# A two-layer relational graph attention kernel: elu's exponential in PSUM, paired transposes of 64-column rests, half-row stores for the last group

## The chip, the cores and the metric

The kernel runs on one core of one Trainium2 chip. The metric is the device time of one execution in microseconds (us). Three runs of the kernel before gave 1726.51, 1728.38 and 1731.38 us, the median 1728.38 us. All traces are of one profiled execution each.

Names of the engines as the profile writes them: PE is TensorE's matmuls, PEld its weight loads, DVE is VectorE, ACT is ScalarE, POOL is GpSimd, SP is SyncE. L12 is line 12 of the kernel before.

## The reference

A graph has 3125 nodes with 768 features each and 53125 edges, sorted by their target node; each edge has one of 3 relations. Two attention layers run over it, then a residual and a layer norm:

```python
def rgat_conv(x, W, q, k, b, src, dst, etype, heads, out_ch, n):
    xr = einsum('nd,rdf->rnf', x, W)          # one product per relation
    oi, oj = xr[etype, dst], xr[etype, src]   # rows of the edges' two ends
    alpha = leaky_relu(oi @ q + oj @ k, 0.2)
    e = exp(alpha - segment_max(alpha, dst)[dst])
    a = e / (segment_sum(e, dst)[dst] + 1e-16)
    return segment_sum(a * oj, dst) + b       # per head
h   = elu(rgat_conv(x, W1, q1, k1, b1, ..., heads=4, out_ch=192))
out = rgat_conv(h, W2, q2, k2, b2, ..., heads=1, out_ch=768)
y   = layernorm(x + out)
```

elu(v) is v for v > 0 and exp(v) - 1 otherwise. The kernel computes it as max(v, 0) + (min(exp(v), 1) - 1).

## The kernel before, in words

**Groups and slots.** The nodes are cut into 25 groups of 128 at most (NB = 25), each with the edges that end in it. A group's edges fill 17 slots of 128 edges (the first group has 14). Of every slot, 128 rows are fetched from a table in HBM by one indirect DMA that POOL issues (`gather_rows`, L485): 422 gathers in each of the two layers.

**Three stages.** Stage 1 makes the table of the first layer (xr for all relations) and the second layer's weights. Stage 2 (`phase2`) is the first aggregation: it gathers rows from `tab1`, sums them by target, applies elu and multiplies h by W2, whose products it stores as rows of `tab2`. Stage 3 (`phase3`) is the second aggregation: it gathers from `tab2`, sums, and ends in layer norm and the store of the output.

**The order of the work** is written out by hand. Each stage makes a list of steps with `when(k, f, ...)`, where k is a place on an axis counted in slots; the list is sorted by k and then emitted. So k sets only the order in which each engine's queue receives its instructions. Every engine works off its queue in that order and waits for what its next instruction needs. The places stand in the tables `STEPS2` and `STEPS3` at the head of the kernel.

**Stage 2, one group b:**

- `alpha`, `turn`, `scan`, `back`, `weigh` and `sums`, in two halves u = 0 and 1 (slots 0 to 7 and 8 on): scores (DVE), their transposes (PE, tile `pa`), running maxima in both directions (DVE, L921 and L923), exponent (ACT, L927), transposes back (PE), the weighted one-hot matrices `sel` (DVE, L963), and the sums by target (PE, tile `acc`). `alpha` is what waits for the gathered rows.
- `e_y` (L1012): divides by the sum of weights and adds the bias: `y`, 128 partitions by 4 windows by 192. Partition 32h + i of window w holds head h of node 32w + i.
- `e_x` (L1023): exp of y on ACT (L1026), into `ey`.
- `e_h` (L1061): three DVE operations (L1063, L1065, L1066): min and minus 1 on `ey` in place; the sum with max(y, 0) for columns 128 to 191 of each window, written a second time behind column 192 of `y`; the same for all 192 columns, in place. So a window's 256 columns hold the 128 first ones, the 64 others, and the 64 others again.
- `h_row` (L1068): four DMAs on SP store h into `tab2`.
- `e_t` (L1078, `turned`, L1034): 8 transposes on PE of 128 columns each into the PSUM tile `pt`: four windows' first 128 columns into its first bank, and four windows' columns 128 to 255 into its second. As the 64 last columns stand there twice, they come out on partitions 0 to 63 and on 64 to 127.
- `e_s`, `e_s2` (`high_parts` L1039, `low_parts` L1050): h is split into a high part (rounded, ACT) and a low part (the remainder, DVE), tile `hT`. For the first bank that is one operation over 128 partitions by 512 on each engine (L1044, L1055), for the second two over 64 partitions by 256 (L1048, L1059).
- `d_products` (L1088): h times W2 in four pieces of 18 matmuls, in two banks `po` by turns; `d_row` (L1112) copies a piece to SBUF (ACT, L1117) and, after the second piece of a row, stores it with one DMA on SP (L1119).

In steady state PE's queue runs: `turn(b, 1)`, the 8 transposes of group b-1, 20 matmuls of group b-2, `back(b, 1)`, 16 matmuls of group b-1, `sums(b, 1)`, `turn(b+1, 0)`, 20 matmuls, `back(b+1, 0)`, 16 matmuls, `sums(b+1, 0)`. DVE's queue runs: `e_h(b-1)`, `alpha(b, 1)`, `scan(b, 1)`, `low_parts(b-1)`, `weigh(b, 1)`, `marks`, `alpha(b+1, 0)`, `scan(b+1, 0)`, `e_y(b)`, `weigh(b+1, 0)`. From group 15 on, 24 steps `move` (L1002, L1003, both DVE) are spread between these; they prepare the row numbers of stage 3. `paced` makes a gather wait until PE has come to a certain place of the order, in stage 2 about 5.5 slots ahead of the gather's own.

**Stage 3, one group b:** the same chain in one half: `a_alpha`, `a_turn`, `a_scan`, `a_exp`, `a_back`, `weigh` at the places `STEPS3["s"]`, counted from the group's last slot, then `sums`. PE also does the products of the group before (`d_part`, tile `D`, seven places from 2.5 on and five from 5.8 on, counted from the same slot): two of these seven lie before place 3.0. The first gather of stage 3 waits for all stores into `tab2`.

Of the kernel before, what the change touches and what calls it, by code (L numbers as in the profile page):

```python
# [21 lines left out]
P = 128  # L22
# [43 lines left out]
def _index(ap):  # L66
# [36 lines left out]
STEPS3 = {"f": -13,  # L103
          "marks": -5,
          "q": (-19, -17.27, -3.5, -2),
          "s": (1.9, 3.0, 3.05, 3.1, 5.6, 5.7, 9.5),
          "round": 0.9,
          "r": (16.7, 16.7, 16.72, 16.75, 19.25, 19.3, 16.71, 16.73, 20.5, 20.6),
          "t": (16.74, 16.78),
# [6 lines left out]
def kernel(  # L116
# [727 lines left out]
    def phase2(work, psum):  # L844
# [166 lines left out]
        def e_y(b):  # L1011
            s = blk[b]  # L1012
            acc = [a[:, :HW].rearrange("p (w f) -> p w f", w=2) for a in s["acc"]]
            rz = work.tile([P, 2, 2], F32, name="rz", bufs=2)
            for c in range(2):
                V.tensor_scalar(rz[:, c], acc[c][:, :, F1], EPS, None, op0=ALU.add)
            V.reciprocal(rz, rz)
            y = s["y"] = work.tile([P, 4, 2 * P], F32, name="y", bufs=1)
            for w in range(4):
                V.scalar_tensor_tensor(y[:, w, :F1], acc[w // 2][:, w % 2, :F1], rz[:, w // 2, w % 2:w % 2 + 1],  # L1020
                                       bias1, op0=ALU.mult, op1=ALU.add)

        def e_x(b):  # L1023
            s = blk[b]
            s["ey"] = work.tile([P, 4, F1], F32, name="ey", bufs=1)
            S.activation(s["ey"], s["y"][:, :, :F1], AF.Exp)  # L1026

        def busy(n):

# [3 lines left out]

        def turned(s, c):  # L1034

            for t in range(4):
                T.transpose(s["pt"][:, c, t * P:(t + 1) * P], s["y"][:, t, c * P:(c + 1) * P], ident)

        def high_parts(s, c):  # L1039

            hT = s["hT"].rearrange("p s t (w i) -> p s t w i", i=32)
            pt = s["pt"][:, c].rearrange("p (w h i) -> p h w i", h=H1, i=32)
            if c == 0:
                S.copy(hT[:, 0, :H1], pt)  # L1044
                return
            for u in range(2):
                p = slice(64 * u, 64 * u + 64)
                S.copy(hT[p, 0, H1:], pt[p, u::2])  # L1048

        def low_parts(s, c):  # L1050

            hT = s["hT"].rearrange("p s t (w i) -> p s t w i", i=32)
            pt = s["pt"][:, c].rearrange("p (w h i) -> p h w i", h=H1, i=32)
            if c == 0:
                V.tensor_sub(hT[:, 1, :H1], pt, hT[:, 0, :H1].bitcast(F32))  # L1055
                return
            for u in range(2):
                p = slice(64 * u, 64 * u + 64)
                V.tensor_sub(hT[p, 1, H1:], pt[p, u::2], hT[p, 0, H1:].bitcast(F32))  # L1059

        def e_h(b):  # L1061
            s = blk[b]
            V.tensor_scalar(s["ey"], s["ey"], 1.0, -1.0, op0=ALU.min, op1=ALU.add)  # L1063
            y, ey = s["y"], s["ey"]
            V.scalar_tensor_tensor(y[:, :, F1:], y[:, :, P:F1], 0.0, ey[:, :, P:], op0=ALU.max, op1=ALU.add)  # L1065
            V.scalar_tensor_tensor(y[:, :, :F1], y[:, :, :F1], 0.0, ey, op0=ALU.max, op1=ALU.add)  # L1066

        def h_row(b):  # L1068

            s = blk[b]  # L1070
            s["rows"] = tab2[b * P * R:(b + 1) * P * R, :].rearrange("(n r) f -> n r f", r=R)
            to = s["rows"][:, WHOLE, :D].rearrange("(w i) (h f) -> h i w f", i=32, h=H1)
            for h in range(H1):
                nc.sync.dma_start(to[h], s["y"][32 * h:32 * h + 32, :, :F1])

        def e_t(b):
            s = blk[b]
# [34 lines left out]
        def d_row(b, p):  # L1112
# [2 lines left out]
            r, c = divmod(p, 2)  # L1115
            n = HW if c == 0 else D + 1 - HW
            S.copy(rows[r][:, c * HW:c * HW + n], po[:, :n])  # L1117
            if c == 1:
                nc.sync.dma_start(s["rows"][:, r, :], rows[r])  # L1119

        def d_tail(b, p):
# [1091 lines left out]
```

## Time and profile before

| what | us |
|---|---|
| median of three runs | 1728.38 |
| the profiled execution, its time | 1726.83 |
| its span, first to last instruction | 1724.9 |
| PE busy (share of the span) | 1640.5 (95%) |
| DVE busy | 1106.6 (64%) |
| POOL busy | 904.8 (52%) |
| ACT busy | 423.8 (25%) |
| mean granted clock of TensorE | 0.979 |

The profiled execution's time is 1.9 us over its span. The span falls into stage 1 (to about 545 us), stage 2 (to about 1128 us), a passage of some 30 us, stage 3 (its gathers run to 1683 us), and a tail. In a row of the timeline the first number is the start in us, the second the time that the row's instructions cover, `xN` their number; the bracket tells how long the engine was idle before and what ended it ("issue" means nothing that the profile shows). In a row of groups the numbers behind the bar are busy us and the mean of one instruction in ns. A matmul's row shows 128 partitions by its columns; the products `D` of stage 3 stand as two records each.

### The profile page before, as it was taken

To read this page: it belongs to the slowest core of one execution; us is meant where nothing else is said; L and a number is where in the kernel's file an instruction comes from. 1 tells how busy PE (TensorE), PEld (TensorE's weight loads), DVE (VectorE), ACT (ScalarE), POOL (GpSimd) and SP (SyncE) were. 2 spreads that over 40 slices of the span, in tenths; PEclk is the share of its full clock that TensorE was granted. 3 is DMA by queue.
4 is the path that set the end of the run, shared out by engine and by line. 5 is a ranking of instruction groups with operands and counts; after the bars stand their busy time and mean duration, and the time that the engine had idled before them with its cause. 6 is when DMAs were issued, how large, how long until landed. Compare 5 with 4: busy or idle time off the path is not lost.

```text
span 1724.9 us, 39077 instructions
## 1 busy us (share of the span) xinstructions
PE 1640.5 (95%) x14233; PEld 1269.5 (74%) x14233; DVE 1106.6 (64%) x4107; ACT 423.8 (25%) x796; POOL 904.8 (52%) x907
## 2 busy tenths in 40 slices
PE   9999999999996999999999999939999999999996
PEld 8999999999995788888888888924444444444443
DVE  5467666676425566666677777465766666666665
ACT  5122222112110111111111111212333333333333
POOL 5100000000007777777777777057777777777770
PEclk9999999999997999999999999969999999999999
DMA  9576766666568999999999999569999999999991
GB/s 329 180 244 210 258 220 210 199 183 203 191 251 281 330 345 355 347 348 348 346 346 356 354 351 351 172 230 324 334 336 340 335 337 338 338 336 340 334 338 39
DMA packets 169368, 500.48 MB, mean 290 GB/s; under 512 B 39891, under 2 KB 82490, under 8 KB 169167
## 3 DMA queue, kind: packets, MB, share of 16 engines
q0 software_dynamic: 70832, 343.91, 56.1%
q1 hardware_dynamic: 90104, 143.89, 25.0%
q10 hardware_dynamic: 8230, 10.10, 1.7%
q8 instruction: 114, 1.87, 0.4%
q14 instruction: 88, 0.71, 0.1%
HBM read 412.96 MB, written 89.63 MB: 291 GB/s over the span
## 4 chain that ended last, share of the span: by engine, by line
PE 69%; DMA 12%; issue 8%; POOL 6%; DVE 4%; ACT 0%; POOLq 0%; DVEq 0%; ACTq 0%; SPq 0%
PE po L56 47%; PE acc L56 13%; PE D L56 4%; DMA waH<-ftab,ridx 3%; DMA waL<-ftab,ridx 3%; POOL waH L485 2%; PE pa L59 2%; PE pt L59 2%; DMA share<-ftab,ridx 1%; DMA extra<-ftab,ridx 1%; POOL waL L485 1%; POOL extra L485 1%; DMA spare_rows<-ftab,ridx 1%; POOL share L485 1%; PE bank L56 1%
## 5 line engine op out<-in xcount | busy, mean ns | idle before, releaser
L485 POOL DMA_INDIRECT extra<-ftab,ridx x296 | 303.3, 1025 | 90.2 <-issue 48.2
L56 PE MATMUL po<-waH,hT 128*128 128x386 f32 (+1 forms) x1200 | 323.1, 344 | 1.0 <-DVE hT L1055 0.8
L56 PE MATMUL po<-waH,xT 128*128 128x386 f32 x1104 | 293.0, 341 | 0.0
L485 POOL DMA_INDIRECT share<-ftab,ridx x209 | 214.2, 1025 | 63.7 <-issue 36.3
L56 PEld LDWEIGHTS po<-waH,hT 128*128 128x128 f32 x1200 | 220.4, 189 | 3.4 <-DVE hT L1055 1.1
L56 PE MATMUL po<-waL,hT 128*128 128x386 f32 (+1 forms) x600 | 207.6, 346 | 0.0
L56 PE MATMUL D<-extra,AT 128*128 128x512 f32 (+1 forms) x576 | 207.2, 503 | 0.0
L56 PEld LDWEIGHTS po<-waH,xT 128*128 128x128 f32 x1104 | 202.4, 189 | 0.5 <-issue 0.4
L56 PE MATMUL po<-waL,xT 128*128 128x386 f32 x552 | 186.9, 339 | 0.0
L598 ACT COPY share<-po 128x386 f32<-128x386 f32 x150 | 72.3, 482 | 371.2 <-PE po L56 298.7
L56 PEld LDWEIGHTS D<-extra,AT 128*128 128x128 f32 x576 | 105.6, 193 | 67.9 <-issue 60.3
L56 PE MATMUL acc<-waL,marks 128*32 128x386 f32 (+1 forms) x860 | 152.8, 490 | 0.0
L56 PE MATMUL po<-wbH,xT 128*128 128x386 f32 (+1 forms) x552 | 147.5, 341 | 1.3 <-DVE wbL L431 1.3
L56 PE MATMUL acc<-waH,marks 128*32 128x384 f32 (+1 forms) x828 | 141.3, 496 | 0.7 <-DVE marks L1359 0.7
L56 PE MATMUL acc<-extra,marks 128*32 128x386 f32 (+1 forms) x564 | 129.5, 487 | 0.0
L485 POOL DMA_INDIRECT waL<-ftab,ridx x108 | 108.1, 1001 | 32.9 <-issue 26.8
L56 PE MATMUL acc<-extra,sel 128*32 128x193 f32 x2736 | 122.6, 331 | 2.3 <-DVE sel L963 2.3
L927 ACT ACTIVATE e<-e 32x128 f32<-32x128 f32 (+2 forms) x50 | 15.5, 310 | 432.9 <-DVE e L926 432.9
L485 POOL DMA_INDIRECT waH<-ftab,ridx x103 | 102.8, 998 | 31.4 <-issue 25.0
L56 PEld LDWEIGHTS po<-waL,hT 128*128 128x128 f32 x600 | 113.7, 190 | 0.6 <-issue 0.3
L762 POOL DMA_DIRECT2D share<-in_L_gnn_W_dram x24 | 12.8, 536 | 188.4 <-DVE w2j L773 117.3
L56 PEld LDWEIGHTS acc<-extra,sel 128*32 128x32 f32 x2736 | 86.7, 111 | 31.4 <-issue 5.8
(312 smaller groups left out, 3078.1 us busy)
## 6 DMA issues: line engine op xcount, KB each, us to landing
ftab<-share SPq DMA_DIRECT2D x150, 193.0 KB
ftab<-r SPq DMA_DIRECT2D x50, 386.0 KB
sT<-dr_d SPq DMA_DIRECT2D x23, 544.0 KB
xb_d<-share SPq DMA_DIRECT2D x25, 384.0 KB
ftab<-y SPq DMA_DIRECT2D x100, 96.0 KB
share<-xb_d SPq DMA_DIRECT2D x25, 384.0 KB
share<-in_x_dram SPq DMA_DIRECT2D x24, 384.0 KB
out_dram<-share SPq DMA_DIRECT2D x24, 384.0 KB
```

Of the source, the lines that this page charges most:

```text
L56: return self.add(self.engine.matmul(to, weights, moving, **more), to, moving)
L59: return self.add(self.engine.transpose(to, a, unit), to, a)
L485: return G.indirect_dma_start(out=to, out_offset=None, in_=tab, in_offset=_index(i[:, j:j + 1]), bounds_check=NP * R - 1, oob_is_err=False)
L598: S.copy(o[:, :HW], po[:, :HW])
L762: G.dma_start(w2[i][p:p + n], l2["W"][r, at:at + n, :])
L927: S.activation(e, e, AF.Exp)
```

## The change

- `e_x`: `ey` lies in PSUM, in the two banks of `pt`, instead of SBUF. `e_h` works on it there.
- `e_h`: the second sum goes to a tile of its own, `rest`, 128 partitions by 256 (four windows by 64); `y` is 192 columns wide.
- `turned`: the rests are transposed two windows at a time: 2 transposes in place of 4, so 6 per group in place of 8. The rest of an even window comes out on partitions 0 to 63, that of an odd one on 64 to 127.
- `high_parts` and `low_parts`: for the rests four operations over 64 partitions by 128 on each engine, in place of two over 64 by 256. Two of the four read one half of the partitions and write the other.
- `d_row`: for the last group every half row is stored by a DMA of its own, as soon as it is copied.
- `STEPS3["s"]`: `a_turn`, `a_scan` and `a_exp` move from places 3.0, 3.05 and 3.1 to 2.2, 2.35 and 2.4.

```diff
-          "s": (1.9, 3.0, 3.05, 3.1, 5.6, 5.7, 9.5),
+          "s": (1.9, 2.2, 2.35, 2.4, 5.6, 5.7, 9.5),
...
-            y = s["y"] = work.tile([P, 4, 2 * P], F32, name="y", bufs=1)
+            y = s["y"] = work.tile([P, 4, F1], F32, name="y", bufs=1)
+            s["rest"] = work.tile([P, 2 * P], F32, name="rest", bufs=1)
...
         def e_x(b):
             s = blk[b]
-            s["ey"] = work.tile([P, 4, F1], F32, name="ey", bufs=1)
-            S.activation(s["ey"], s["y"][:, :, :F1], AF.Exp)
+            ey = psum.tile([P, 2, 512], F32, name="pt", bufs=1)
+            s["ey"] = ey.rearrange("p c (w f) -> p (c w) f", w=2)[:, :, :F1]
+            S.activation(s["ey"], s["y"], AF.Exp)
...
         def turned(s, c):
 
-            for t in range(4):
-                T.transpose(s["pt"][:, c, t * P:(t + 1) * P], s["y"][:, t, c * P:(c + 1) * P], ident)
+            if c == 0:
+                for t in range(4):
+                    T.transpose(s["pt"][:, 0, t * P:(t + 1) * P], s["y"][:, t, :P], ident)
+                return
+            for t in range(2):
+                T.transpose(s["pt"][:, 1, t * P:(t + 1) * P], s["rest"][:, t * P:(t + 1) * P], ident)
+
+        def rests(s, k):
+
+            hT = s["hT"].rearrange("p s t (m q i) -> p s t m q i", q=2, i=32)
+            pt = s["pt"][:, 1, :2 * P].rearrange("p (m t u i) -> p t m u i", m=2, u=2, i=32)
+            for u in range(2):
+                for q in range(2):
+                    yield hT[64 * u:64 * u + 64, k, H1:, :, q], pt[64 * q:64 * q + 64, :, :, u]
...
-            for u in range(2):
-                p = slice(64 * u, 64 * u + 64)
-                S.copy(hT[p, 0, H1:], pt[p, u::2])
+            for to, rest in rests(s, 0):
+                S.copy(to, rest)
...
-            for u in range(2):
-                p = slice(64 * u, 64 * u + 64)
-                V.tensor_sub(hT[p, 1, H1:], pt[p, u::2], hT[p, 0, H1:].bitcast(F32))
+            for (to, rest), (high, _) in zip(rests(s, 1), rests(s, 0)):
+                V.tensor_sub(to, rest, high.bitcast(F32))
...
-            V.scalar_tensor_tensor(y[:, :, F1:], y[:, :, P:F1], 0.0, ey[:, :, P:], op0=ALU.max, op1=ALU.add)
-            V.scalar_tensor_tensor(y[:, :, :F1], y[:, :, :F1], 0.0, ey, op0=ALU.max, op1=ALU.add)
+            V.scalar_tensor_tensor(s["rest"].rearrange("p (w f) -> p w f", w=4), y[:, :, P:], 0.0, ey[:, :, P:], op0=ALU.max, op1=ALU.add)
+            V.scalar_tensor_tensor(y, y, 0.0, ey, op0=ALU.max, op1=ALU.add)
...
             S.copy(rows[r][:, c * HW:c * HW + n], po[:, :n])
-            if c == 1:
+            if b == NB - 1:
+                f = slice(c * HW, (c + 1) * HW)
+                nc.sync.dma_start(s["rows"][:, r, f], rows[r][:, f])
+            elif c == 1:
                 nc.sync.dma_start(s["rows"][:, r, :], rows[r])
```

More of the change, by code (lines that the diff above doesn't have):

```diff
@@ L1017, in e_y @@
             V.reciprocal(rz, rz)
-            y = s["y"] = work.tile([P, 4, 2 * P], F32, name="y", bufs=1)
+            y = s["y"] = work.tile([P, 4, F1], F32, name="y", bufs=1)
+            s["rest"] = work.tile([P, 2 * P], F32, name="rest", bufs=1)
             for w in range(4):
-                V.scalar_tensor_tensor(y[:, w, :F1], acc[w // 2][:, w % 2, :F1], rz[:, w // 2, w % 2:w % 2 + 1],
+                V.scalar_tensor_tensor(y[:, w], acc[w // 2][:, w % 2, :F1], rz[:, w // 2, w % 2:w % 2 + 1],
                                        bias1, op0=ALU.mult, op1=ALU.add)
@@ L1073, in h_row @@
             for h in range(H1):
-                nc.sync.dma_start(to[h], s["y"][32 * h:32 * h + 32, :, :F1])
+                nc.sync.dma_start(to[h], s["y"][32 * h:32 * h + 32])
         def e_t(b):
```

## The prediction

> **What bounds the kernel now.** I read the page's slices first, then the busy time by stage.
>
> ```profile
> span 1724.9 us, 39077 instructions
> ...
> PE   9999999999996999999999999939999999999996
> ```
>
> ```profile
> 602.00:1128.00 526.00, 525.44 (x6076) 455.74 (x6076) 358.60 (x1106) 99.74 (x232) 371.48 (x361) 1.00 0.93 331
> 658.00:680.80 22.80, 22.80 (x278) 19.66 (x274) 14.83 (x49) 4.26 (x10) 17.47 (x18) 1.00 0.97 362
> 1131.00:1683.00 552.00, 509.45 (x3768) 240.68 (x3770) 372.09 (x1686) 184.21 (x307) 422.64 (x422) 0.96 0.94 332
> ```
>
> The columns are length, then busy us of PE, PEld, DVE, ACT and POOL, granted clock, DMA share, GB/s. From 602 to 1128 us PE has work all the time: stage 2 is as long as what stands in PE's queue. In stage 3 PE has 42 us without work, so something else sets its length. POOL's rows by themselves tell what:
>
> ```profile
> 519.67:1083.21 563.54, 435.21 (x422) 0.98 0.96 344
> 1131.84:1682.86 551.02, 422.64 (x422) 0.96 0.94 332
> ```
>
> Length, POOL busy, clock, DMA share and GB/s for the gathers alone. Between two gathers POOL is idle 0.30 us (rows below), so 422 gathers that never wait take 422 x 0.30 more than their busy time: 549 us in stage 3, and it lasts 551. Stage 3 is as long as POOL's issues: whatever is spared or added inside it shows only in its tail. In stage 2 the same sum is 562 of 563.5 us, so POOL looks like a bound there too. The timeline of one group shows why it is none:
>
> ```profile
> 835.91 1.00 POOL L485 DMA_INDIRECT share<-ftab,ridx  x1 [0.30 <-issue]
> 837.21 1.64 POOL L485 DMA_INDIRECT share<-ftab,ridx  x1 [0.30 <-DVE y L1065]
> ```
>
> ```profile
> 859.99 1.61 POOL L485 DMA_INDIRECT share<-ftab,ridx  x1 [0.30 <-DVE y L1065]
> ```
>
> ```profile
> 837.02 0.96 DVE L1066 SCALAR_TENSOR_TENSOR y<-y,ey 128x768 f32<-128x768 f32 x1
> ```
>
> 17 gathers of 1.30 us are 22.1, and one in each group is stretched by 0.64 under elu's large sum on DVE: 22.74, while the group lasts 859.99 - 837.21 = 22.78 us. Every group POOL gains 0.64 on PE and is held by 0.64 at the same DVE instruction; it is locked to PE's pace. Free of that it could go at 22.1 us a group. So stage 2 is PE's, stage 3 POOL's.
>
> **Fewer transposes.**
>
> ```profile
> L59 PE MATMUL pt<-fident,y x200: 270/273/273, 565.1 to 1111.2; 128*128 128x128 f32 x100
> ```
>
> ```profile
> 841.03 1.04 PE L59 MATMUL pt<-fident,y 128*128 128x128 f32 x8
> ```
>
> Eight transposes cover 1.04 us and one lasts 0.273, so one starts every (1.04 - 0.27) / 7 = 0.11 us. Two fewer spare PE 0.22 us a group. PE is the bound from 602 us on; groups 2 to 24 have their transposes after that: 23 x 0.22 = **-5.0 us**. POOL and DMA must then keep 22.55 us a group; POOL can, and the row 658 to 680.8 shows DMA at 362 GB/s where 22.55 us asks for about 1% more than now.
>
> **elu in PSUM.** What DVE's three operations then cost is bounded by these rows:
>
> ```profile
> L390 DVE COPY t<-pt 128x768 f32<-128x768 f32 x3 | 2.9, 957 | 2.9 <-PE pt L59 2.9
> ...
> L1420 DVE SCALAR_TENSOR_TENSOR share<-acc,half,share 128x768 f32<-128x768 f32 x50 | 50.3, 1007 | 1.7 <-ACT share L1415 0.8
> ...
> L1063 DVE TENSOR_SCALAR ey<-ey 128x768 f32<-128x768 f32 x25 | 14.3, 571 | 0.9 <-ACT ey L1026 0.9
> ```
>
> The first operation goes from 0.57 to 0.96 us at most (the copy of 768 columns from PSUM); the large sum from 0.96 to 1.01 (the sum with one operand in PSUM). Operations on PSUM overlap the next one's start, so I take +0.25 us a group, between 0 and +0.45. ACT's exp into PSUM has no row of its own; it ends while DVE is still at `sel`, so it is free. What hides the 0.25 is DVE's lead over the next turn on PE. Where the moves stand in between, there is none left:
>
> ```profile
> 931.99 0.18 DVE L907 COPY near<-al 64x28 f32<-64x28 f32 x1
> ```
>
> ```profile
> 932.23 0.29 PE L59 MATMUL pa<-fident,near 128*36 128x128 f32 x1
> ```
>
> That transpose starts when DVE is done. For this group and its neighbours from 16 on, and the turn that follows the rests' longer work, I charge **+0.5 us** together (0 to 1.2).
>
> The gain on POOL: in the row L1420 above one operand lies in SBUF and one in PSUM, and 50 such sums leave stage 3's gathers at 422.64 / 422 = 1.00 us. Stage 2's took 435.21, so 14 us of stretch stand there, most of it at elu. The Trainium skill, SBUF — State Buffer, section Who interferes with whom, says that a VectorE instruction with two inputs in SBUF contends with a GpSimd instruction that reads SBUF, and one with at most one such input does not; the trace agrees (1.64 against 1.00 us). Taken alone, that rule would make POOL's freedom worth up to the 14 us. PE's row says it is worth something only before 602 us, where PE still waits for rows. There the chain of waits reads
>
> ```profile
> 594.38 7.15 DMA extra<-ftab,ridx
> ```
>
> and ahead of this gather four were stretched under elu:
>
> ```profile
> 559.26 1.25 POOL L485 DMA_INDIRECT share<-ftab,rfirst  x1 [0.30 <-issue]
> 560.81 1.15 POOL L485 DMA_INDIRECT share<-ftab,rfirst  x1 [0.30 <-PE acc L56]
> ```
>
> ```profile
> 583.44 1.38 POOL L485 DMA_INDIRECT share<-ftab,ridx  x1 [0.30 <-PE po L56]
> 585.12 1.15 POOL L485 DMA_INDIRECT share<-ftab,ridx  x1 [0.30 <-issue]
> ```
>
> 0.25 + 0.15 + 0.38 + 0.15 = **-0.9 us** (0 to -1.2).
>
> **The rests in four pieces.** ACT copies them, DVE waits for ACT's last copy, subtracts, and then makes `sel`, for which PE's sums wait:
>
> ```profile
> 843.59 0.75 ACT L1048 CAST hT<-pt 64x256 fp32r<-64x256 f32 x2
> ```
>
> ```profile
> 844.37 0.69 DVE L1055 TENSOR_TENSOR hT<-pt,hT 128x512 fp32r<-128x512 f32 x1 [1.56 <-ACT hT L1048]
> 844.98 0.85 DVE L1059 TENSOR_TENSOR hT<-pt,hT 64x256 fp32r<-64x256 f32 x2
> ```
>
> ```profile
> 845.85 2.02 DVE L963 TENSOR_TENSOR sel<-marks,pa 128x1152 f32<-128x1152 f32 x3
> ```
>
> ```profile
> 848.72 2.17 PE L56 MATMUL acc<-extra,sel 128*32 128x193 f32 x48
> ```
>
> A piece of 64 by 128 has no row. Above it lies that of 64 by 256 (0.37 on ACT, 0.42 on DVE); nearest are operations of 128 columns:
>
> ```profile
> L416 ACT COPY sm<-bank 128x128 f32<-128x128 f32 x9 | 2.4, 266 | 12.0 <-PE bank L56 12.0
> ```
>
> ```profile
> L926 DVE TENSOR_TENSOR e<-pa,B 32x128 f32<-32x128 f32 x25 | 7.0, 278 | 0.9
> ```
>
> The two halves of a row here do not overlap (2 x 0.37 = 0.75, 2 x 0.42 = 0.85), so I let four pieces not overlap either: ACT 4 x 0.28 = 1.1 (+0.37), DVE 4 x 0.29 = 1.18 (+0.33). `sel` comes 0.70 us later, PE 0.22 earlier: 0.92 in all. `sel` is done at 847.87 and its sums start at 848.72, a slack of 0.85. It is more than that, since the sums need only the first of the three instructions at their start. The group at 909 us shows it, where moves stand ahead of `sel`:
>
> ```profile
> 914.76 0.60 DVE L1003 TENSOR_TENSOR pall<-pall 128x425 f32<-128x425 f32 x1
> 915.40 2.02 DVE L963 TENSOR_TENSOR sel<-marks,pa 128x1152 f32<-128x1152 f32 x3
> ```
>
> ```profile
> 917.12 0.37 PE L56 MATMUL acc<-share,sel 128*32 128x193 f32 x4
> ```
>
> `sel` ends at 917.42, 0.30 us after its sums began, and PE did not wait. So an ordinary group has 0.85 + 0.30 = 1.15 us, and 0.92 fits. In a group with a move at this place nothing is left, and PE loses most of the 0.92: 0.8. Such groups are three, with L1003 at 914.76, 960.64 and the last at
>
> ```profile
> 1006.11 0.60 DVE L1003 TENSOR_TENSOR pall<-pall 128x425 f32<-128x425 f32 x1
> ```
>
> 3 x 0.8 = **+2.4 us** (0, if DVE no longer waits for ACT's last copy, to 3).
>
> **The last half rows.** The chain into stage 3 is
>
> ```profile
> 1128.25 2.64 DMA ftab<-r
> ```
>
> ```profile
> ftab<-r SPq DMA_DIRECT2D x50, 386.0 KB
> ```
>
> The last store then carries half the bytes, and the first half is gone before. At the 362 GB/s above, 386 KB need 1.07 of the 2.64 us, so half of them spares 0.5 at most; smaller rows may eat some of it. I take **-0.2 us** (+0.1 to -0.6). SP has two more issues, in gaps while it waits for ACT.
>
> **Turn before the two products.** In stage 3 PE today does two products of the group before, then waits for the scores:
>
> ```profile
> 1666.26 0.27 PE L59 MATMUL pa<-fident,al 128*17 128x128 f32 x1 [0.88 <-DVE al L1313]
> ```
>
> From place 2.2 the turn comes first. It still starts when the rows have landed, and the two products, until now inside the wait, follow it. POOL hides this for all groups but the last. In the tail the chain reads
>
> ```profile
> 1685.77 1.82 PE D L56 x4
> 1687.59 0.22 PE pa L59 x2
> 1687.81 3.87 PE D L56 x10
> ```
>
> Ten records last 3.87, so four cost 1.55, at most 1.82. Behind the turn of group 23, held by its rows, they push everything after it: **+1.6 us** (0 to 2.2). DVE's and ACT's orders stay as they are, and an earlier scan finds PE busy with seven products in place of five.
>
> **Sum.** -5.0 + 0.5 - 0.9 + 2.4 - 0.2 + 1.6 = -1.6 us: 1726.83 to 1725.2 for the profiled execution, which lies 1.55 under the median; on the median 1728.38 that is **1726.8 us**. About 0.3% (5.2 us) is what a measurement here can tell from no change.
>
> **Rivals.**
>
> - *The delays cost nothing.* DVE takes the low parts of the first bank while ACT still copies the rests, and the products behind the turn find another gap: -5.0 - 0.9 - 0.2 = -6.1, 1722.3. For it: the low parts of the first bank need no rests. Against: today's bracket on L1055. 16%.
> - *POOL paces stage 2 after all*, and PE's busy rows hide waits. Freed of some 10 of its 14 us, with the tail's +1.6: 1720. For it: POOL's sum of 562 in 563.5. Against: a matmul that waits shows a gap, and PE shows none. 8%. (It is what the Trainium skill's rule above would give if the gathers alone counted.)
> - *PE's gain is not taken up*, because POOL stays locked (the backward scan too has two operands in SBUF) or DMA is full: 3.4 us over the median, 1731.8. 5%.
> - *Slower: the four pieces cost as much each as the two do now.* Then `sel` is 0.75 + 0.85 = 1.6 later against 1.15 of slack: PE waits 0.45 in each of 23 groups, +10 in place of -5.0 and of the 2.4, with the rest (+1.0) 1739. It decides from about 0.37 us for a piece. For it: two pieces cross from one half of the partitions to the other, for which no PSUM row stands. Against: the 0.27 and 0.28 above. 7%.
>
> **How the numbers follow.** The forecast keeps 64%; its own range runs from 1724 to 1730. The 8-in-10 range takes in the first and the third rival and leaves out the last and most of the second: 1721.5 to 1731.8. Faster by over 0.3% are the first two rivals, 24%; slower the last and a little more, 8%; within, 68%.
>
> **What would show it.** Six transposes of `y` and `rest` a group; gathers in stage 2 near 1.00 us, with no 1.6; the group at 22.55 us until 870 us; three waits of PE for `sel` near 917, 963 and 1008 us; in the tail 14 records of D behind the turn. A group at 22.78 us again would refute the main term, gaps ahead of `acc` in every group would show the last rival, and a tail as short as before would refute the term of the turn.

## The result and the profile after

The changed kernel's median is 1724.99 us over 22 runs (1723.11 to 1728.39), that of the kernel before on the same chips 1728.17 us (1725.15 to 1733.69). The ratio is 0.9984 with a 95% interval of 0.9977 to 0.9991: by the ratio about 2.8 us less, within 0.3%. The forecast was 1.6 us less.

The profiled execution of the changed kernel took 1727.58 us, its span is 1725.8: 0.9 us *more* than the profile of before. The spans must not be compared as they stand. The first gather of stage 2 starts at 523.13 us in place of 519.67; the change touches nothing ahead of it, and further profiles have it anywhere from 519.1 to 525.3. So I compare from that gather on:

| stretch | before | after | difference | forecast |
|---|---|---|---|---|
| first gather of stage 2 to the transposes of group 2 (run-in) | 93.39 | 92.12 | -1.27 | -0.9 |
| those of group 2 to those of group 24 | 497.33 | 495.42 | -1.91 | -1.9 |
| those of group 24 to the first gather of stage 3 | 21.44 | 20.31 | -1.13 | -0.4 |
| gathers of stage 3 | 551.02 | 550.06 | -0.96 | 0 |
| last gather's end to the end (tail) | 42.08 | 44.75 | +2.67 | +1.6 |
| sum | 1205.26 | 1202.66 | -2.60 | -1.6 |

(The forecast of the second row is 22 groups by -0.22, plus 2.9 of delays; two more transposes are in the third.) The windows of after, with the columns of before's:

```profile
602.00:1128.00 526.00, 523.66 (x6098) 454.34 (x6086) 374.64 (x1155) 106.75 (x278) 365.85 (x362) 1.00 0.94 334
660.40:682.96 22.56, 22.56 (x270) 19.42 (x269) 15.86 (x51) 4.58 (x12) 17.19 (x18) 1.00 1.00 365
1131.00:1683.00 552.00, 509.37 (x3762) 242.10 (x3764) 372.53 (x1681) 183.28 (x306) 421.67 (x422) 0.96 0.94 332
```

One group takes 22.56 us in place of 22.80 and PE is busy in all of it. The gathers alone (length, POOL busy, clock, DMA share, GB/s):

```profile
523.13:1082.71 559.58, 426.42 (x422) 0.98 0.97 346
1130.98:1681.04 550.06, 421.68 (x422) 0.96 0.94 333
```

Stage 2's gathers are 9 us less busy than before's 435.21. For the group shown in the prediction, POOL's timeline now has

```profile
837.64 1.00 POOL L485 DMA_INDIRECT extra<-ftab,ridx  x1 [0.30 <-DVE rest L1077]
...
849.61 1.16 POOL L485 DMA_INDIRECT extra<-ftab,ridx  x1 [0.55 <-PE acc L56]
```

The gather beside elu lasts 1.00 us in place of 1.64, and once in this group POOL waits for PE: 0.55 us idle, where the gap between gathers is 0.30. Such waits begin late: the first gap over 0.35 us is

```profile
827.06 1.15 POOL L485 DMA_INDIRECT share<-ftab,ridx  x1 [0.60 <-PE acc L56]
```

and there are ten up to 1050 us, nine of them ended by PE. Ahead of 827 us POOL never waits: 17 gathers take 22.1 to 22.4 us, while PE's groups take 22.55 to 22.60. So POOL gains a lead first, and PE holds it only when it has that lead.

The new operations, by tile `pt` (shortest, median, longest in ns):

```profile
L1061 ACT CAST hT<-pt x100: 255/260/265, 571.6 to 1112.8; 64x128 fp32r<-64x128 f32 x100
L1071 DVE TENSOR_TENSOR hT<-pt,hT x100: 271/288/298, 573.3 to 1114.6; 64x128 fp32r<-64x128 f32 x100
...
L1075 DVE TENSOR_SCALAR pt<-pt x25: 954/958/965, 563.3 to 1107.1; 128x768 f32<-128x768 f32 x25
```

A piece of the rests costs 0.26 us on ACT and 0.29 on DVE; elu's first operation went from 0.57 to 0.96 us. PE's waits behind DVE, none of which before had from 610 us on:

```profile
916.78 4.22 PE L56 MATMUL acc<-share,sel 128*32 128x193 f32 x96 [0.50 <-DVE sel L963]
932.33 0.29 PE L59 MATMUL pa<-fident,near 128*36 128x128 f32 x1 [0.21 <-DVE near L907]
```

```profile
963.20 0.54 PE L56 MATMUL acc<-extra,sel 128*32 128x193 f32 x8 [0.58 <-DVE sel L963]
```

```profile
1009.03 0.53 PE L56 MATMUL acc<-share,sel 128*32 128x193 f32 x8 [0.50 <-DVE sel L963]
```

with a last one for `near` at 1069.69 (0.26). The gaps add up to 2.05 us, but the groups lose more: matmuls in a row overlap when nothing holds them, so a wait costs more than the gap that it leaves. The transpose at 932.33 starts 0.50 us behind the one ahead of it, where the transposes in the prediction start 0.11 apart. Against 22.57 us the four groups with these waits take 23.74, 23.31, 23.26 and 23.00, 3.0 us more in all: 2.2 at `sel` and 0.8 at `near`. The first of them seen from DVE: four pieces, a move, and only then `sel`:

```profile
912.98 1.18 DVE L1071 TENSOR_TENSOR hT<-pt,hT 64x128 fp32r<-64x128 f32 x4
914.20 0.50 DVE L1002 TENSOR_SCALAR pall<-ridx,first_row,moved 128x425 f32<-128x425 int32 x1
914.73 0.60 DVE L1003 TENSOR_TENSOR pall<-pall 128x425 f32<-128x425 f32 x1
915.37 2.02 DVE L963 TENSOR_TENSOR sel<-marks,pa 128x1152 f32<-128x1152 f32 x3
```

And the turn of group 23 with the 14 records of D behind it:

```profile
1665.12 0.27 PE L59 MATMUL pa<-fident,al 128*17 128x128 f32 x1 [0.32 <-DVE al L1328]
1665.62 0.28 PE L59 MATMUL pa<-fident,next 128*17 128x128 f32 x1 [0.23 <-DVE next L1330]
1665.74 5.75 PE L56 MATMUL D<-extra,AT 128*128 128x512 f32 x14
1671.42 0.23 PE L59 MATMUL pa<-fident,e 17*128 17x17 f32 x1
```

Most of the experiments (e1 to e4, e5 and e6, e8 to e11) ran on three chips on which the kernel before takes 1959 to 1986 us, because the gathered rows come in more slowly there; each kernel is compared with the kernel before on its own chip. Line numbers in a row are those of the run's own kernel.

### The profile page after: what moved, and what is told of

Read it like the earlier page. It is cut to its first block, busy times and chain, and to the rows that moved or that the text cites. A ratio compares the mean times of both kernels' runs of the same rounds, so it can differ in the third digit from the quotient of the medians.

```text
span 1725.8 us, 39081 instructions
## 1 busy us (share of the span) xinstructions
PE 1638.3 (95%) x14183; PEld 1267.9 (73%) x14183; DVE 1124.9 (65%) x4157; ACT 431.3 (25%) x846; POOL 894.6 (52%) x907
## 4 chain that ended last, share of the span: by engine, by line
PE 72%; DMA 8%; issue 7%; DVE 6%; POOL 5%; ACT 1%; POOLq 0%; DVEq 0%; ACTq 0%; SPq 0%
PE po L56 46%; PE acc L56 15%; PE D L56 7%; DMA extra<-ftab,ridx 2%; POOL waH L485 2%; DMA waL<-ftab,ridx 2%; PE pa L59 2%; POOL extra L485 1%; PE pt L59 1%; DMA waH<-ftab,ridx 1%; POOL waL L485 1%; DMA spare_rows<-ftab,ridx 1%; POOL share L485 1%; DMA share<-ftab,ridx 1%; DVE junk L1317 1%
## 5 line engine op out<-in xcount | busy, mean ns | idle before, releaser
L485 POOL DMA_INDIRECT extra<-ftab,ridx x296 | 297.6, 1005 | 92.9 <-issue 49.7
L56 PE MATMUL D<-extra,AT 128*128 128x512 f32 (+1 forms) x576 | 202.3, 502 | 0.0
L485 POOL DMA_INDIRECT waL<-ftab,ridx x108 | 107.8, 998 | 32.9 <-issue 26.8
L485 POOL DMA_INDIRECT waH<-ftab,ridx x103 | 102.8, 998 | 31.4 <-issue 26.8
```

The source lines that it names most:

```text
L56: return self.add(self.engine.matmul(to, weights, moving, **more), to, moving)
L485: return G.indirect_dma_start(out=to, out_offset=None, in_=tab, in_offset=_index(i[:, j:j + 1]), bounds_check=NP * R - 1, oob_is_err=False)
```

## The experiments

**How long the gathers hold stage 2 on those three chips.** In a stretch of stage 2 e9 (first row) moves 299 GB/s, the profile of before (second) 349, in columns as above:

```profile
700.00:1150.00 450.00, 418.65 (x4542) 345.30 (x4540) 283.66 (x885) 77.37 (x204) 289.16 (x288) 1.00 0.91 299
```

```profile
680.00:1050.00 370.00, 370.00 (x4382) 319.23 (x4375) 263.32 (x810) 70.23 (x165) 285.87 (x277) 1.00 0.97 349
```

PE is idle for 31 of 450 us. POOL's waits in e8 (us in total, times, longest) have an entry that neither before nor after has:

```profile
POOL extra L485 <- remote: 45.1, 41, 1.9
POOL share L485 <- remote: 33.3, 28, 1.9
```

All ten profiles from these chips have this entry, the four of the other chips (before, after, e7, e12) have none. It names no engine of the core; what holds the gathers there, the trace does not say. A group takes 26.8 to 27.3 us there, so what the change spares on PE is lost in waits for rows. Those runs tell about single operations, the passage to stage 3 and the tail, not about PE's or POOL's pace.

**e2 and e11: elu in PSUM alone** (before, with this edit only):

```diff
-            s["ey"] = work.tile([P, 4, F1], F32, name="ey", bufs=1)
+            ey = psum.tile([P, 2, 512], F32, name="pt", bufs=1)
+            s["ey"] = ey.rearrange("p c (w f) -> p (c w) f", w=2)[:, :, :F1]
```

> The kernel before with one edit: the exponential of elu lies in PSUM. Eight transposes, two pieces for the rests, whole rows and the late turn stay. Theory A: PE paces stage 2, and POOL was only locked to it. Then the 9 us of stretch under elu's large sum go, gaps in which POOL waits for PE come in their place, and the group stays at 22.78 to 22.80 us; only the run-in gains, from the first gather to the transposes of group 2, 92.1 to 92.5 us in place of 93.39; time 1727 (1 us under before). Theory B: POOL paces stage 2 and PE's busy rows hide waits. Then the group falls to 22.2 to 22.4 us and the time to 1715 to 1720. Theory C: the longer operations on DVE delay the turns in the groups with moves: waits for near in the second half of stage 2, up to 0.5 us in all.

> The kernel before with one edit: the exponential of elu lies in PSUM. Theory A: PE paces stage 2, POOL is only locked to it. Then the 9 us of stretch under elu's large sum go, waits of POOL for PE come in their place, the group stays at 22.78 to 22.80 us, and only the run-in gains, 92.1 to 92.5 us from the first gather to the transposes of group 2 in place of 93.39. Time 1 us under before. Theory B: POOL paces stage 2. Then the group falls to 22.2 to 22.4 us and the time to 8 to 12 us under before.

Measured: 1986.39 us against 1985.55, ratio 0.9997 (0.9981 to 1.0014); 1958.31 against 1959.11, 0.9990 (0.9976 to 1.0003). Elu's stretch of the gathers is gone in both. The groups are at 27.2 and 26.8 us, so theories A and B are not told apart. Neither profile has a wait for `near` from 600 us on, so theory C shows nothing here either.

**e3 and e8: elu in SBUF, all else as changed** (the same edit, undone in the changed kernel).

> The changed kernel with one edit undone: the exponential of elu lies in SBUF again, six transposes stay. Theory A: the stretch under elu is only what is left over between POOL and PE, and gets shorter when PE gets faster. Then the group is at 22.57 us as in the changed kernel, the stretch under elu's large sum falls from 0.64 to about 0.43 us a group, and only the run-in is lost: 93.0 to 93.4 us from the first gather to the transposes of group 2 in place of 92.12; time 1 us over the changed kernel, 1726. Theory B: POOL holds PE back by the stretch, and the saving on PE needs elu out of SBUF. Then the group stays at 22.74 to 22.78 us, gathers show 1.6 us as before, and the time is 4 to 5 us over the changed kernel, about 1729.5.

> The changed kernel with the exponential of elu in SBUF again; six transposes stay. Theory A: POOL's stretch under elu is only what is left over between POOL's own 22.1 us and PE's group, and gets shorter when PE gets faster. Then the group is at 22.57 us as in the changed kernel, with about 0.45 us of stretch under elu in each in place of 0.64, and only the run-in is lost: 93.0 to 93.4 us from the first gather to the transposes of group 2 in place of 92.12. Time 1 us over the changed kernel. Theory B: POOL holds PE back by the stretch, and the saving on PE needs elu out of SBUF. Then the group stays at 22.74 to 22.78 us, gathers of 1.6 us stay, and the time is 4 to 5 us over the changed kernel, 1 us over before.

Measured: 1982.07 against 1985.55, 0.9987 (0.9971 to 1.0003); 1957.16 against 1959.11, 0.9980 (0.9967 to 0.9993). Groups at 27.2 and 26.8 us: nothing told apart. e12 has the same edit.

**e12: elu in SBUF, moves at idle places, late turn for the last two groups** (the edit of e3, and these).

```diff
-          "move": 3.3,
+          "move": (9.02, 17.52, 17.57),
...
+          "last": (1.9, 3.0, 3.05, 3.1, 5.6, 5.7, 9.5),
...
-            when(base(late) + STEPS2["move"] + i * (NB - 1 - late) * SL / (NB - 2), move, i + 1)
+            when(base(late + i // 3) + STEPS2["move"][i % 3], move, i + 1)
...
-            for k, f in zip(t["s"], (a_alpha, a_turn, a_scan, a_exp, a_back, weigh)):
+            for k, f in zip(t["s" if b < NB - 2 else "last"], (a_alpha, a_turn, a_scan, a_exp, a_back, weigh)):
```

> The changed kernel with three edits: the 24 moves at the places where DVE waits for PE anyway (three in each of groups 15 to 22), the late turn for the last two groups of stage 3 alone, and the exponential of elu in SBUF again. Where DMA leaves room: for the third edit, theory A: POOL's stretch under elu is what is left over between POOL's 22.1 us and PE's group. Then the group is at 22.57 us as in the changed kernel, the stretch under elu is about 0.45 us in each, and only the run-in is lost, 93.0 to 93.4 us from the first gather to the transposes of group 2 in place of 92.12. Theory B: POOL holds PE back by the stretch; then the group stays at 22.74 to 22.78 us with gathers of 1.6 us. For the others: no wait of PE for DVE in stage 2, a tail of 42.1 to 42.8 us, a stretch of 0.7 us in stage 3's gathers. By A the time is 6.5 to 7 us under before, by B 2 to 3.

Measured, on a chip like that of the first profiles: 1726.20 us over 12 runs against 1729.63, 0.9978 (0.9963 to 0.9993), by the ratio 3.8 us less. Theory A had put the time 6.5 to 7 us under before; that is missed, and theory A is judged by its group and its stretch. In stage 2 PE is without a gap from 658 to 1080 us:

```profile
658.00:1080.00 422.00, 422.00 (x4996) 363.44 (x4998) 312.09 (x980) 86.32 (x226) 325.42 (x318) 1.00 0.98 352
```

Groups 5 to 22 take 22.55 to 22.60 us with elu in SBUF. The gathers beside elu, and the DVE rows over them:

```profile
840.72 1.24 POOL L486 DMA_INDIRECT share<-ftab,ridx  x1 [0.31 <-issue]
842.26 1.15 POOL L486 DMA_INDIRECT share<-ftab,ridx  x1 [0.30 <-issue]
```

```profile
840.52 0.55 DVE L1075 TENSOR_SCALAR ey<-ey 128x768 f32<-128x768 f32 x1
...
841.57 0.96 DVE L1078 SCALAR_TENSOR_TENSOR y<-y,ey 128x768 f32<-128x768 f32 x1
```

The stretch is 0.24 + 0.15 = 0.39 us where before it was 0.64. Theory A holds: the stretch is what is left over between POOL's own pace and PE's, and shrinks with PE's group. It leaves POOL without reserve: its gathers take 562.14 us and it never waits for PE, so late rows are not caught up; PE waits for them at 654.12 (0.90) and 1083.74 us (0.45), and group 4 takes 23.75. From the transposes of group 2 to those of group 24 e12 takes 494.54 us where e7, with the same moves and elu in PSUM, takes 492.35 (one profile each). The run-in is 93.16 us, as A had it.

The tail is 44.21 us, not 42.1 to 42.8. The order did what was expected: from group 23's turn to the next transposes of `A` it took 18.32 us, against 20.15 after. What is longer is the last stretch of D, at a lower granted clock (length, PE busy, clock):

```profile
1707.44:1718.01 10.57, 9.40 (x46) 0.84 0.01 3
```

In e7 the same stretch takes

```profile
1700.30:1709.40 9.10, 7.84 (x46) 1.00 0.02 5
```

1.5 us lie in the clock; without them the tail is 42.7. Six of twelve experiment profiles have it at 0.84 to 0.95 there, with either order; what lowers it is open.

**e1 and e9: the late turn again** (stage 3's places of before) in the changed kernel.

```diff
-          "s": (1.9, 2.2, 2.35, 2.4, 5.6, 5.7, 9.5),
+          "s": (1.9, 3.0, 3.05, 3.1, 5.6, 5.7, 9.5),
```

> The changed kernel with stage 3's turn, scan and exponent back at the places 3.0, 3.05 and 3.1; all else as changed. Measured from the last gather's end to the end of the span (the tail), before had 42.08 us and the changed kernel 44.75; from the first to the last gather of stage 3 they had 551.02 and 550.06. Theory A, the prediction's: the earlier turn costs the tail alone, and POOL hides it elsewhere. Then the tail is 42.1 to 42.8, the gathers stay near 550.1, and the time falls by 1.6 to 2.7 us against the changed kernel, to about 1722.8. Theory B: the earlier turn is also what took 0.9 us of stretch from the gathers under the backward scan (1.28 before, 0.34 after). Then the tail is 42.1 but the gathers take 551.0 again, the stretch under that scan is back near 1.3, and the net is -1.7, about 1723.3. Theory C: the tail hangs on when the last rows land, which scatters; then it stays at 44 or more and the time at 1725.

> The changed kernel with stage 3's turn, scan and exponent back at 3.0, 3.05 and 3.1. Theory A: the early turn costs the tail alone. Then the tail after the last gather is 42.1 to 42.8 us in place of 44.75, the stretch of stage 3's gathers stays near 0.7 us, and the time is 2 us under the changed kernel. Theory B: the early turn also spared the gathers 0.9 us of stretch under the backward scan. Then the tail is the same, but the stretch is back at 1.6 us, and the time is 1 to 1.3 us under the changed kernel.

Measured: 1985.19 against 1985.55, 0.9997 (0.9982 to 1.0012); 1955.74 against 1959.11, 0.9987 (0.9973 to 1.0000). The numbers of the expectations cannot be met there: the last turn comes 15 to 17 us after the last gather, in place of 4.6 to 5.4 on the other chips, and the tails are 54.10 and 54.65 us, against 56.14 to 56.94 in e3, e4, e6 and e8 with the early turn. Part of those 2 us is the clock (e2, with the late turn and the low clock, has 56.28). PE's time from the last turn to its sums is 6.69 to 6.70 us in every profile with the late turn and 8.61 or more with the early one. That shows the order, and is no loss by itself: the early order has in this stretch the four records that the late one has ahead of the turn. What the order costs the tail is shown by e7 and e12, on chips like that of after. The gathers' stretch under the backward scan shows nothing where POOL waits for its queue.

**e5: late turn and elu in SBUF** (both edits from above).

> The changed kernel with two edits undone that lie in different stages: the exponential of elu lies in SBUF again (stage 2), and stage 3's turn, scan and exponent are back at 3.0, 3.05 and 3.1. Where DMA leaves room, as in the profiles of before and of the changed kernel: stage 2, theory A: the stretch under elu is only what is left over between POOL and PE; then the group is at 22.57 us with about 0.43 us of stretch under elu's large sum in each. Theory B: POOL holds PE back by the stretch; then the group is at 22.74 to 22.78 us. Stage 3, theory A: the early turn cost the tail alone; then the tail after the last gather is 42.1 to 42.8 us in place of 44.75, and the gathers stay near 550.1. Theory B: it also spared POOL stretch; then the gathers take 551.0 with 1.3 us of stretch under the backward scan. By A and A the time is that of the changed kernel less 1 us (tail -2, run-in +1).

Measured: 1977.83 against 1980.25, 0.9991 (0.9973 to 1.0009). The group is at 27.2 us and the tail at 54.01: the tail is as short as in e1, the rest is as in e3.

**e4: low parts of the first bank ahead of the rests' high parts.**

```diff
         def e_s(b):
-            for c in range(2):
-                high_parts(blk[b], c)
+            high_parts(blk[b], 0)
+            low_parts(blk[b], 0)
+            high_parts(blk[b], 1)
...
         def e_s2(b):
-            for c in range(2):
-                low_parts(blk[b], c)
+            low_parts(blk[b], 1)
```

> The changed kernel with the low parts of the first bank ahead of the high parts of the rests in the order, so that DVE's subtraction over 128 by 512 waits for ACT's first copy alone and no longer for the fifth. Everything computed as before. DVE can then start 0.61 us earlier after the transposes, but its four pieces still wait for ACT's last copy at 3.62 us behind the transposes: sel ends 0.6 us earlier (its first instruction 6.2 us behind the transposes in place of 6.84). Theory A: the three waits of PE for sel at 916.78 (0.50), 963.20 (0.58) and 1009.03 us (0.50) come from the four pieces. Then all three go, the groups after them fall from 23.74, 23.31 and 23.26 to about 23.1, 22.6 and 22.6 us, and the time falls by about 1.8 us, to 1723.2. Theory B: the moves alone make these waits, or the wait for near behind them takes their place; then the groups stay at 23.2 or more and the time at 1725.

Measured: 1979.66 against 1985.55, 0.9980 (0.9961 to 0.9999), but the edit did not do what I wrote. ACT and PE in one group:

```profile
959.83 1.07 ACT L1061 CAST hT<-pt 64x128 fp32r<-64x128 f32 x4 [0.76 <-DVE hT L1068]
960.92 0.48 ACT L1129 COPY r<-po 128x386 f32<-128x386 f32 x1
```

```profile
961.46 0.44 PE L56 MATMUL po<-waH,hT 128*128 128x386 f32 x1 [0.95 <-ACT r L1129]
```

ACT's four pieces now wait for DVE's subtraction, DVE's pieces wait for ACT, and nothing overlaps: the four pieces on DVE end 0.28 us later in the last group (4.51 in place of 4.23 behind its transposes). ACT's copy of a finished bank moves back with them, and PE waits ahead of its products: 24.4 us in 21 waits from 680 to 1210 us, where e1 has 7.0 in 18 and e3 6.4 in 17. (For 8 of the 21, 8.3 us, the profile names ACT's copy as what ended them; for the rest it names nothing.) The waits for `sel` do shrink, as theory A has it, to 0.5 us in 3 where e1 has 3.2 in 6 and e3 2.6 in 4, but far more is added ahead of the products. So this edit does not hide the pieces; what it would do where rows come in time was not measured. Its ratio lies within the interval of e3's, on the same chip, and has no cause shown.

**e6: the same, and whole rows for the last group.**

```diff
-            if b == NB - 1:
-                f = slice(c * HW, (c + 1) * HW)
-                nc.sync.dma_start(s["rows"][:, r, f], rows[r][:, f])
-            elif c == 1:
+            if c == 1:
```

> The changed kernel with two edits in different places: the low parts of the first bank stand ahead of the high parts of the rests in the order (DVE starts them 0.6 us earlier), and the last group's rows are stored whole again. Where DMA leaves room: theory A for the first edit: PE's waits for sel (0.50, 0.58 and 0.50 us near 917, 963 and 1009 us) go, and the groups after them take 22.6 to 23.1 us in place of 23.74, 23.31 and 23.26; theory B: moves or the wait for near keep them at 23.2 or more. For the second: from the last transposes of stage 2 to the first gather of stage 3 before took 21.44 us and the changed kernel 20.31, of which two transposes are 0.22. Theory A: the half rows made the other 0.9, and whole rows bring 21.2. Theory B, the prediction's size: they made 0.2, the rest is scatter of one store, and it stays at 20.5 or less.

Measured: 1976.62 against 1980.25, 0.9982 (0.9965 to 1.0000). The group's last transposes and the first gather of stage 3 in e6:

```profile
1248.53 0.60 PE L59 MATMUL pt<-fident,y 128*128 128x128 f32 x4
```

```profile
1269.76 0.99 POOL L485 DMA_INDIRECT waH<-ftab,rfirst  x1 [51.08 <-DMA f<-ed_d]
```

That is 21.23 us. With half rows it is 20.31 to 20.39 in ten profiles on at least five chips (20.31 in e4, which differs from e6 by the half rows alone and ran on another chip), with whole rows and eight transposes 21.40 to 21.44 in three. The half rows spare 0.9 us: theory A. The first edit shows as in e4: PE waits 24.5 us in 19 waits ahead of its products.

**e10: moves at idle places and the late turn for the last two groups** (e12 with elu in PSUM).

> The changed kernel with the 24 moves at the places where DVE waits for PE anyway (three in each of groups 15 to 22), and with the late turn for the last two groups alone. Theory A: both gains add up: no wait of PE from 602 us to the end of stage 2's products (-2.9 us), a tail of 42.1 to 42.8 us in place of 44.75 (-2), gathers of stage 3 with 0.7 us of stretch. Then the time is 4.5 to 5 us under the changed kernel and 7.5 to 8 under before, a ratio of 0.9955. Theory B: the tail hangs on the order of all groups, not of the last two; then it stays at 44 and the time is 3 us under the changed kernel.

Measured: 1956.10 against 1959.11, 0.9989 (0.9972 to 1.0006). The tail is 54.09 us, as short as with the late turn in all groups: the last two groups decide, and theory B falls. From 600 us to the end of stage 2 PE waits neither for `sel` nor for `near`. The sum of the gains cannot show there.

**e7: moves at idle places, late turn in all groups.**

> The changed kernel with two edits in different stages. Stage 2: the 24 moves on DVE are no longer spread evenly over groups 15 to 24, but stand three to a group in groups 15 to 22 at places where DVE waits for PE anyway: behind each of the two turns ahead of its scan, and behind the second scan ahead of the low parts. Stage 3: turn, scan and exponent are back at 3.0, 3.05 and 3.1. Where DMA leaves room, theory A: PE's five waits behind DVE (0.50, 0.21, 0.58, 0.50 and 0.26 us at 916.78, 932.33, 963.20, 1009.03 and 1069.69) all go, every group from 3 to 23 takes 22.55 to 22.6 us, and from the transposes of group 14 to those of group 24 it takes 221.6 us in place of 224.55; the tail is 42.1 to 42.8 us in place of 44.75. Together 5 us under the changed kernel, about 1720. Theory B: a move ahead of a scan delays the transposes of the exponents instead, and PE waits there, about 0.3 us in each of the eight groups, so that nothing is won in stage 2; and the early turn had spared stage 3's gathers 0.9 us, so that the time is 1723.5. Where DMA holds the rows back, as in the profiles of e1 to e6, the first part shows nothing and the tail falls by 2.4 us.

Measured, one run on a chip like that of the first profiles: 1722.22 us against one run of the kernel before, 1726.54, 4.3 less. PE has no gap at all:

```profile
658.00:1080.00 422.00, 422.00 (x4995) 363.74 (x4992) 319.43 (x982) 86.05 (x226) 321.82 (x317) 1.00 0.98 352
```

while after had 2.09 us of gaps in the same 422. From the transposes of group 14 to those of group 24 it takes 221.48 us in place of 224.55. A move fits where DVE waits for ACT:

```profile
907.97 0.49 DVE L1002 TENSOR_SCALAR pall<-ridx,first_row,moved 128x425 f32<-128x425 int32 x1
908.49 0.61 DVE L1003 TENSOR_TENSOR pall<-pall 128x425 f32<-128x425 f32 x1
909.93 0.69 DVE L1068 TENSOR_TENSOR hT<-pt,hT 128x512 fp32r<-128x512 f32 x1 [0.83 <-ACT hT L1061]
```

So the delays came from the moves ahead of the longer pieces, 3.07 us in all. The tail is 42.82, 1.93 us shorter. Two things went the other way: stage 3's gathers took 552.15 us, 2.1 more than in after, and the run-in 93.54. About 0.9 of the 2.1 is stretch (1.61 in place of 0.70); the rest is 3 to 4 ns more for each gather. The median gather takes 1.002 us in e7, e10 and e12, the three kernels with the moves at other places, and 0.998 in the other eleven profiles; why is open. From the first gather of stage 2 to the end e7 takes 1201.17 us, 1.5 less than after in these two profiles, where 5 were expected. One run of e7 against one of before is no measurement of the time, and whether e10 beats e7 where rows come in time was not measured.

## Why the prediction was right, step by step

- **Bounds.** Right. PE paces stage 2: freed of the stretch, POOL does 17 gathers in 22.1 to 22.4 us until 827 us and then waits for PE, while PE's groups stay at 22.57 up to the first group with a wait for `sel`. That removes the rival *POOL paces stage 2*. Stage 3 stayed as long as POOL's issues.
- **Fewer transposes, -5.0.** Right: the group fell by 0.22 us, from 22.80 to 22.57 on the mean of groups 3 to 14, and DMA kept up at 365 GB/s. The rival *PE's gain is not taken up* is settled by e12: it is taken up with elu in SBUF as well. DMA can still take it: in three profiles (after, e7, e12) it did.
- **elu in PSUM.** DVE's three operations cost 0.39 us more, not 0.25 (inside the bound of 0.45). The two waits for `near` cost 0.8 us where I charged 0.5; how much of that is elu and how much the rests, no run separates. The gathers run at 1.00 us beside elu, as the row with one operand in PSUM said, and the rule of the Trainium skill that the prediction quotes (SBUF — State Buffer, section Who interferes with whom) agrees there. But the prediction left out a condition of that rule: the section says that a VectorE instruction with at most one input in SBUF does not contend *outside the 2-port perf modes*, and names `tensor_scalar` among the operations that can enter such a mode. The prediction's own rows show why it matters: of its four stretched gathers in the run-in, those at 559.26 and 583.44 us lost 0.25 and 0.38 us under L1063, which has one input. In which mode it ran the trace does not say. In the run-in POOL is spared 1.2 us where I had 0.9: the stretch in the first 56 gathers is 1.75 and 1.68 us with elu in SBUF (before, e12), 0.49 and 0.51 in PSUM (after, e7). Where PE stands then scatters by more: 92.12 us in after and 93.54 in e7 to group 2. So it is shown for POOL, not for the time.
- **The rests, +2.4.** Right in mechanism and size: 2.2. A piece costs 0.26 and 0.29 us against 0.28 and 0.29; `sel` comes 0.67 us later against 0.70; ordinary groups hide it, the three groups named wait. With the waits for `near` it is 3.0 us by the groups and 3.07 by e7, forecast 2.9. *The delays cost nothing* and *the pieces cost as much as now* both fall by these rows.
- **The last half rows, -0.2.** Mis-sized: 0.9. The step that failed is "At the 362 GB/s above, 386 KB need 1.07 of the 2.64 us": the store at the end of stage 2, which stands alone, did not go at the rate of many transfers. The wait for it, of whole rows in e6 and of half rows in after:

```profile
1268.99 0.98 ACT L1297 ACTIVATE qd<-fident,q2f 128x128 f32<-128x128 f32 x3 [2.82 <-DMA ftab<-r]
```

```profile
1130.32 0.99 ACT L1300 ACTIVATE qd<-fident,q2f 128x128 f32<-128x128 f32 x3 [2.01 <-DMA ftab<-r]
```

  0.81 us for 193 KB less is about 240 GB/s, an estimate from these two waits; before, with whole rows on a chip like that of after, has 2.85.
- **Turn ahead of two products, +1.6.** Right in place, under in size: 1.92 us behind the turn of group 23 (18.23 to 20.15 us until the next transposes of `A`). Four records more are 1.7, and D waits 0.2 more for `next`. Another 0.67 of the tail lies ahead of that turn: the rows of group 23 were used 6.23 us after their last gather, before 5.56; this scatters (5.3 to 6.2 in the last groups of e7 and e12 in which PE waited for it). With the late turn the tail is 42.82 in e7 and 42.7 in e12 without its clock, not quite before's 42.08. "POOL hides this for all groups but the last" held.
- **Stage 3's gathers.** The sum has no term for them; they took 0.96 us less, nearly all of it stretch under the backward scan (1.28 to 0.34). The four profiles of chips where rows come in time have 1.63 and 1.61 us of stretch with the late turn (before, e7), 0.70 and 1.00 with the early one (after, e12, but for its last two groups). They agree with an effect of the order, and are too few to show it.

So the mechanisms held, and that the total came out so near is in part luck: the half rows spared 0.7 us more than forecast and the tail lost 1.1 more, which nearly cancel. What is left of the 1.0 us between -1.6 and -2.6 in the two profiles are the run-in (-0.4) and stage 3's gathers (-1.0).

## What to carry to other kernels

Where PE has no gap, as here, an instruction fewer on PE is worth the interval at which such instructions start, in every group (two transposes, 0.22 us). An engine that looks as full as PE may only be locked to it: look at what stretches it, and whether that shrinks. Longer work on a side engine cost nothing here until something else stood in the same slack, so look for the few groups where a side job comes between, and put that job where the engine waits anyway. Cut a profile at fixed events before summing differences: here the span alone had the wrong sign.

## What the runs showed of the hardware that I had not expected

- A gather on POOL is stretched by an operation on DVE with inputs in SBUF that began at least 0.05 us before it and still runs 0.13 us after its start: it gets longer by that operation's end less the gather's start, less 0.13 us. At 837.21 before, DVE ended at 837.98: 0.77 - 0.13 = 0.64. At 842.26 in e12, DVE ended at 842.53: 0.27 - 0.13 = 0.14, measured 0.15. An operation with one input in SBUF (L1075, 840.52 to 841.07) did it too: 0.35 - 0.13 = 0.22, measured 0.24. In the 138 such cases of elu's operations in all fourteen profiles the sum is right within 0.02 us. Where the operation began later, from 0.044 us before the gather's start to 0.2 after it, the gather kept its 1.00 us in all 47 cases: the one at 835.91 in before, for which L1063 began at 835.97 and ran for 0.55 us, is one. So a few hundredths of a us decide: in before, the gather at 883.23, 0.06 us behind such an operation, lost 0.77 us, and the one at 1065.13, 0.04 us behind, lost nothing.
- The same kernel takes 1726 to 1730 us on some chips and 1959 to 1986 on others. The stages that gather make the difference: the gathers of e1 take 697 and 660 us where those of after take 560 and 550, while the first gather starts at 521 and 523 us and the passage to stage 3 takes 20.31 in both. There the order of PE's and DVE's work hardly matters: the ten ratios are 0.998 to 1.000. Why the rows come more slowly is open.
- ACT's and DVE's operations that read one PSUM tile and write different places of one SBUF tile were put one behind the other in e4, as soon as the order interleaved them: ACT waited 0.76 us for DVE's subtraction, and in the last group DVE 1.14 us for ACT's copies. Whether the chip needs that, or only the program asks for it, e4 does not show.
